# A pre-norm transformer block on one core: spline parts in the score banks, and the second norm's transpose on VectorE

## The chip, the cores and the metric

The kernel runs on one core of one Trainium2 chip. The metric is the device time of one execution in microseconds (us); a change is judged by the median of several runs of each kernel.

## The reference: what is computed

The input is 16 sequences of 256 tokens with 256 features, in 32-bit floats. One block of a transformer is computed: a layer norm, attention with 16 heads of 16 features each and a window mask, a residual sum, a second layer norm, and a gated feed-forward layer whose three weights (256 x 1024) are rebuilt from about two thousand control points each by cubic interpolation ("spline").

```python
n = layernorm(x)
q, k, v = n @ wq.T, n @ wk.T, n @ wv.T           # 16 heads of 16
s = q @ k.T * 16 ** -0.5                          # per head, 256 x 256
s = where(j - i > 16, -inf, s)
x = x + (softmax(s) @ v) @ wo.T
n = layernorm(x)                                  # the second norm
gate_w, up_w, down_w = (spline_reconstruct(cp) for cp in (gate_cp, up_cp, down_cp))
x = x + (silu(n @ gate_w.T) * (n @ up_w.T)) @ down_w.T
```

## The kernel before, in words

**Steps.** One sequence is one batch entry b, 0 to 15. The kernel walks through 20 steps s, and each step works on several sequences at different stages: the projections of b = s + 3, the row maxima of the scores of nb = s - 1, the exponentials and values of tb = s - 2, the output projection, residual and second norm of ob = s - 3, and most of the feed-forward layer of s - 4. All instructions of an engine are kept in program order (class `InOrder`; its helper line is line 88, so nearly all rows of the profile carry L88 and are told apart by their tiles). Nothing reorders them: the loop at the end of `block_kernel` writes the order out by hand, with gaps 1 to 7 of each step, at which `project(s, gap)` and `fill(s, gap)` put other work between the score stages. The dictionary `early` deals the work of the first steps (0 to 4) to those gaps: the first norm's transposes (`turn_a`), the projections and the weights' spline.

**Scores.** Two tiles, `scores0` and `scores1`, hold two PSUM banks each, so four of the eight banks. `inner` and `outer` fill them for four heads at a time: once without a mask for the maxima (TensorE, then VectorE's `find_max`, whose rows are `z` and `mx`), and once, for the sequence one step older, for the exponentials (ScalarE, rows `e`, then a mask by GpSimd). A step holds four `inner` and two `outer` stages. `turn_max` transposes the maxima (`pm`) and sends them into the q/k tile of the next step by SyncE's DMA queue.

**Other PSUM.** Pool `ps_f` (tag "f", two banks) holds the feed-forward products `pg`, `pu` and `pd`, and pool `ps_m` (tag "m", two banks) the projections `pq`, `pk`, `pv`, `py`, the values `po` and all transposes (`pta`, `ptf`, `pm`).

**The second norm.** `project_o` adds the attention's output to x (rows `x<-x,py`). `norm_stats` takes mean and variance on VectorE (`statsf`, `mvf`) and the inverse root on GpSimd (`rstdf`, power -0.5). `normed` writes `xnf` (two VectorE instructions). `turn_f` transposes it: `transposed` runs four TensorE transposes of 128 x 128 into a PSUM tile `ptf` and one ScalarE copy to `x2T`. `gate_up(b, 0)`, the next step's first feed-forward product, reads `x2T` whole as its moving operand; it stands at gap 7, the end of the step, and its first matmul is `pg`. In steps 4 to 12, TensorE has between the `outer` stage and that `pg`: `down(1)` (`pd`, 16 records), `ptf`, `project_v` (`pv`) and `pm`. From step 13 on there is no `project_v` any more, and `down` is dealt in halves (`fill`), so that `pd` for column block 0 has only one half ahead of `outer`. The sum `x<-x,pd` on VectorE releases each `pd` bank.

**The spline.** `spline(w, part)` makes half of one weight: four matmuls `pw` of 32 rows each into four PSUM banks (two of `ps_f`, two of `ps_m`), then per half a ScalarE copy of the first piece and a VectorE `copy_predicated` of the second over it. Six parts: (gate, 0), (up, 0), (gate, 1), (up, 1), (down, 0), (down, 1). Before, they stand at (step, gap) (0, 4), (1, 5), (1, 7), (2, 6), (2, 7) and (2, 7).

Of the kernel before, what the change touches and what calls it, by code (L numbers as in the profile page):

```python
# [11 lines left out]
F32 = mybir.dt.float32  # L12
BF16 = mybir.dt.bfloat16
AF = mybir.ActivationFunctionType
ALU = mybir.AluOpType
# [3 lines left out]
P = 128  # L19
B, S, DIM = 16, 256, 256  # L20
# [4 lines left out]
EPS = 1e-5  # L25
# [4 lines left out]
NPART = NROW // 2  # L30
# [63 lines left out]
def block_kernel(  # L94
# [14 lines left out]
    pe, dve, act, pool, sp = (  # L109
        InOrder(tc, e) for e in (nc.tensor, nc.vector, nc.scalar, nc.gpsimd, nc.sync)  # L110
    )

    const = ctx.enter_context(tc.tile_pool(name="const", bufs=1))
    sb = ctx.enter_context(tc.tile_pool(name="sb", bufs=2))
    sb1 = ctx.enter_context(tc.tile_pool(name="sb1", bufs=1))
    sb3 = ctx.enter_context(tc.tile_pool(name="sb3", bufs=3))
    sb4 = ctx.enter_context(tc.tile_pool(name="sb4", bufs=4))
# [4 lines left out]
    ps_f = ctx.enter_context(tc.tile_pool(name="ps_f", bufs=2, space=PSUM))  # L122
    ps_m = ctx.enter_context(tc.tile_pool(name="ps_m", bufs=2, space=PSUM))
# [48 lines left out]
    neghalf = const.tile([P, 2], F32, tag="neghalf", name="neghalf")  # L172
# [42 lines left out]
    xns, mxs, aus, aos, recs, x2s, x2Ts = ({} for _ in range(7))  # L215
    es, inters, qkcs = {}, {}, {}

    moments = {}

    def norm_stats(b, nm):  # L220
        stats = sb.tile([P, 2, 6], F32, tag=f"stats{nm}", name=f"stats{nm}{b}")
        mv = sb.tile([P, 2, 2], F32, tag=f"mv{nm}", name=f"mv{nm}{b}")
        for c in range(2):
            dve.bn_stats(stats[:, c, :], xs[b][:, c, :])
            dve.bn_aggr(mv[:, c, :], stats[:, c, :])
        rstd = sb4.tile([P, 2], F32, tag=f"rstd{nm}", name=f"rstd{nm}{b}")
        dve.tensor_scalar_add(rstd, mv[:, :, 1], EPS)
        pool.tensor_tensor(rstd, rstd, neghalf, ALU.pow)
        moments[b, nm] = mv, rstd

    def normed(b, nm):
# [9 lines left out]
    def copied(engine, dst, src):  # L241
        (act.copy if engine is act else dve.tensor_copy)(dst, src)

    def transposed(src, dst, nm, engine=act):

        pt = ps_m.tile([P, 2, S], F32, tag="m", name=f"p{nm}")
        for kc in range(2):
            for c in range(2):
                pe.transpose(
                    pt[:, kc, c * P : (c + 1) * P],  # L250
                    src[:, c, kc * P : (kc + 1) * P],
                    ident,
                )
        copied(engine, dst, pt)


    def stats_a(b):
        norm_stats(b, "a")
# [6 lines left out]
    def norm_a(b):  # L265
        xns[b] = normed(b, "a")

    def turn_a(b, engine=act):
        xTs[b] = sb3.tile([P, 2, S], F32, tag="xT", name=f"xT{b}")
        transposed(xns.pop(b), xTs[b], f"ta{b}", engine)  # L270
# [61 lines left out]
                    qks[b % NQK][32 * r : 32 * r + HD, :, gg::2, :], qkc[at : at + HD]  # L332
                )

    def project_v(b, engine=act, chunks=(0, 1)):
        pv = ps_m.tile([P, 2, DIM], F32, tag="m", name=f"pv{b}")
        for c in chunks:
            for kc in range(2):
                pe.matmul(
                    pv[:, c, :],  # L340
                    lhsT=xTs[b][:, kc, c * P : (c + 1) * P],
                    rhs=w_in["v"][:, kc, :],
                    start=(kc == 0),
                    stop=(kc == 1),
                )
        for c in chunks:
            to = vs[b % NQK][:, c, :, 0:HD]
            heads = pv[:, c, :].rearrange("p (h d) -> p h d", d=HD)
            if b < RAW:
                copied(engine, to, heads)  # L350
            else:
                act.activation(to, heads, AF.Copy, scale=factors[b][:, c : c + 1])
        if 1 in chunks:
            del xTs[b]
# [6 lines left out]
    tiles = [  # L361
        ps_s.tile([P, 2, 512], F32, tag=f"s{pr}", name=f"scores{pr}") for pr in range(2)
    ]
# [185 lines left out]
    def norm_f(b):  # L549
        x2s[b] = normed(b, "f")  # L550

    def turn_f(b):
        x2Ts[b] = sb.tile([P, 2, S], F32, tag="x2T", name=f"x2T{b}")
        transposed(x2s.pop(b), x2Ts[b], f"tf{b}")

    def product(out, lhsT, rhs, start, stop, columns=P):

# [66 lines left out]
            ALU.mult, ALU.mult,  # L624
        )

    def spline(w, part):
        at = slice(NPART * part, NPART * part + NPART)
        places = tab_in[:, NPART + P * part : NPART + P * part + P]

        pw = [
            pool_.tile([P, NPART], F32, tag=tag, name=f"pw{w}_{part}_{kc}_{piece}")
            for kc, (pool_, tag) in enumerate(((ps_f, "f"), (ps_m, "m")))
            for piece in range(2)
        ]
        for q in range(4):
            rows = slice(32 * q, 32 * q + 32)
            pe.matmul(
                pw[q], lhsT=places[rows], rhs=cp_in[rows, w, :], start=True, stop=True
            )  # L640
        for kc in range(2):
            first, other, where = pw[2 * kc], pw[2 * kc + 1], second_in[:, kc, at]
            if w < 2:
                to = (gateT, upT)[w][:, kc, at]
            else:

                to = downT[:, kc::2, NPART // 4 * part : NPART // 4 * (part + 1)]
                first, other, where = (
                    t.rearrange("p (o q) -> p q o", q=4) for t in (first, other, where)
                )  # L650
            act.copy(to, first)
            dve.copy_predicated(to, where, other)

    def do(stage, b, *args):
        if 0 <= b < B:
            stage(b, *args)

    parts = ((0, 0), (1, 0), (0, 1), (1, 1), (2, 0), (2, 1))
# [6 lines left out]
    def fill(s, gap):  # L665


        if s < B - AHEAD:
            order = (
                (1, gate_up, 1, 32), (3, gate_up, 2), (4, gate_up, 3, 32), (5, down, 0),  # L670
                (6, down, 1),
            )
        else:
            order = (
                (1, gate_up, 1, 32), (2, gate_up, 2), (3, gate_up, 3), (4, down, 0, 0, 32),
                (5, down, 0, 1), (6, down, 1, 0), (6.5, down, 1, 1),
            )
        for at, stage, *what in order:
            if at == gap:
                if s == B + 3 and stage is down:  # L680

                    if what[1] == 0:
                        down(B - 1, what[0])
                else:
                    do(stage, s - 4, *what)
        if gap == 7:
            do(gate_up, s - 3, 0)

    def part(i):
        spline(*parts[i])

    early = {
        (0, 1): ((stats_a, 1), (value_ones, 1)),
# [1 line left out]
            (norm_a, 1), (project_qk, 0), (spread, 0), (load_rest, 0), (coefficients, 0),  # L697
            (stats_a, 2), (scores_and_values, 2),
        ),
        (0, 4): ((turn_a, 1, dve), (project_v, 0, dve), (norm_a, 2), (part, 0)),  # L700
        (1, 1): ((turn_a, 2), (project_part, 1, 0), (stats_a, 3)),
        (1, 2): ((project_part, 1, 1), (spread, 1), (coefficients, 1)),
        (1, 3): ((project_qk, 2), (spread, 2), (norm_a, 3), (scores_and_values, 3)),
        (1, 4): ((project_v, 1), (stats_a, 4)),
        (1, 5): ((turn_a, 3), (part, 1), (norm_a, 4), (coefficients, 2)),
        (1, 6): ((project_qk, 3),),
        (1, 7): (
            (spread, 3), (stats_a, 5), (norm_a, 5), (project_v, 2), (part, 2),
            (scores_and_values, 4),
        ),  # L710
        (2, 1): ((turn_a, 4), (turn_a, 5), (scores_and_values, 5)),
        (2, 2): ((project_part, 4, 0), (stats_a, 6)),
        (2, 3): ((project_part, 4, 1), (spread, 4), (project_part, 5, 0)),
        (2, 4): ((norm_a, 6), (project_v, 3, act, (0,))),
        (2, 5): ((project_part, 5, 1), (spread, 5)),
        (2, 6): ((project_v, 3, act, (1,)), (part, 3)),
        (2, 7): ((part, 4), (part, 5)),
        (3, 1): ((turn_a, 6),),
        (3, 2): ((project_qk, 6), (spread, 6)),
        (3, 3): ((project_v, 4), (project_v, 5)),  # L720
        (3, 6): ((project_v, 6), (sum_weights, "q"), (sum_weights, "k")),
        (3, 7): ((center, "q"), (center, "k")),
        (4, 1): ((sum_weights, "v"), (center, "v")),
    }

    def project(s, gap):
# [22 lines left out]
    minus_ones(1)  # L749
    stats_a(0)  # L750
    norm_a(0)
    turn_a(0)
    for s in range(B + 4):
        nb, tb, ob = s - 1, s - 2, s - 3
        inner(nb, tb, 0)
        if ob < B - 1:
            do(values, ob, 1)
            do(gather, ob)
        project(s, 1)
        fill(s, 1)  # L760
        inner(nb, tb, 1)
        do(invert, ob)
        if s:
            do(load_x, s + 2 + AHEAD)
        project(s, 2)
        fill(s, 2)
        outer(nb, tb, 0)
        project(s, 3)
        fill(s, 3)
        inner(nb, tb, 2)  # L770
        do(values, tb, 0)
        project(s, 4)
        do(divide, ob)
        fill(s, 4)
        inner(nb, tb, 3)
        do(project_o, ob)
        do(stats_f, ob)
        project(s, 5)
        fill(s, 5)
        if s != 3:  # L780
            do(norm_f, ob)
        outer(nb, tb, 1)
        fill(s, 6)
        if s == 3:

            project(s, 6)
            norm_f(ob)
            turn_max(nb)
        do(turn_f, ob)
        if s != 3:  # L790
            project(s, 6)
        fill(s, 6.5)
        if tb == B - 1:
            values(tb, 1)
            gather(tb)
        if s != 3:
            do(turn_max, nb)
        project(s, 7)
        fill(s, 7)
# [30 lines left out]
```

## Time and profile before

| what | value |
|---|---|
| median of 3 runs | 651.25 us (650.94 to 652.86) |
| the profiled execution: its own time | 652.13 us |
| its span in the profile | 650.4 us |
| TensorE (PE), matmul busy | 642.7 us, 99% |
| VectorE (DVE) busy | 369.2 us, 57% |
| ScalarE (ACT) busy | 216.4 us, 33% |
| GpSimd (POOL) busy | 129.5 us, 20% |
| mean granted TensorE clock | 0.997 |

The span runs from the first to the last instruction of the program; 1.7 us of the profiled execution lie around it. Busy TensorE time is partly modelled: matmuls overlap, so what a stage costs is read from the starts of its first instruction and of the next stage's first one, not from the instructions' durations. A row of the timeline gives start, length, engine, operation, tiles written and read, count, and in brackets the idle time before it with what ended it.

### The profile page before, as it was taken

What the parts mean: (1) busy time and instruction counts of PE and PEld (TensorE: products, weight loads), DVE (VectorE), ACT (ScalarE), POOL (GpSimd) and SP (SyncE); (2) the same over time, 40 slices, a digit from 0 to 9 for tenths busy, and PEclk for the clock granted to TensorE, in tenths of its full rate; (3) what the DMA queues carried; (4) which work ended last, traced back from release to release, by engine and by line L of the source; (5) the groups of instructions that cost most, each with busy time, mean ns of one, the idle gap of its engine ahead of it and who ended that gap; (6) DMA issues with size and microseconds to landing.
All of it is one profiled execution on the core that took longest, in us unless ns stands there. A gap on an engine that the chain in (4) does not pass through costs nothing.

```text
span 650.4 us, 21144 instructions
## 1 busy us (share of the span) xinstructions
PE 642.7 (99%) x8740; PEld 477.3 (73%) x8740; DVE 369.2 (57%) x1483; ACT 216.4 (33%) x383; POOL 129.5 (20%) x254
## 2 busy tenths in 40 slices
PE   8999999999999999999999999999999999999998
PEld 7666667777778777787877778777777777777777
DVE  6785566646465664646566464655656565633342
ACT  1345543233332323333232332323333333333110
POOL 6232222111121211212112121211212030312000
PEclk9999899999999999999999999999999999999999
DMA  5843141414132131312213131210010101010100
GB/s 173 174 69 54 35 83 29 82 38 86 34 76 42 35 75 39 86 35 69 49 31 80 36 72 34 54 32 21 19 36 20 36 21 30 26 41 14 51 17 17
DMA packets 40768, 33.36 MB, mean 51 GB/s; under 512 B 10593, under 2 KB 40033, under 8 KB 40673
## 3 DMA queue, kind: packets, MB, share of 16 engines
q1 hardware_dynamic: 39392, 30.90, 21.7%
q8 instruction: 69, 1.13, 0.8%
q10 hardware_dynamic: 1280, 1.11, 0.6%
q14 instruction: 27, 0.21, 0.3%
HBM read 14.42 MB, written 4.47 MB: 29 GB/s over the span
## 4 chain that ended last, share of the span: by engine, by line
PE 96%; DMA 1%; DVE 1%; ACT 1%; issue 1%; POOL 0%; SPq 0%; ACTq 0%
PE pg L88 18%; PE pd L88 17%; PE pu L88 17%; PE scores L88 15%; PE po L88 7%; PE py L88 5%; PE pq L88 4%; PE pk L88 4%; PE pv L88 4%; PE pw L88 1%; PE ptf L88 1%; DMA qk<-qkc 1%; DMA x<-x 1%; PE pm L88 1%; PE pta L88 0%
## 5 line engine op out<-in xcount | busy, mean ns | idle before, releaser
L88 ACT ACTIVATE e<-scores 128x512 f32<-128x512 f32 (+1 forms) x192 | 117.5, 615 | 268.9 <-PE scores L88 222.6
L88 DVE CUSTOM_DVE_ANT_0 z<-scores,mask 128x144 bf16<-128x144 f32 (+1 forms) x512 | 154.7, 362 | 56.0 <-PE scores L88 33.3
L88 POOL TENSOR_SCALAR_AFFINE_SELECT e<-e 128x224 f32<-128x224 f32 (+1 forms) x192 | 93.8, 489 | 403.0 <-ACT e L88 402.6
L88 PE MATMUL pg<-x2T,gateT 128*32 128x256 f32 (+1 forms) x1112 | 124.0, 381 | 0.7 <-ACT x2T L88 0.7
L88 PE MATMUL pu<-x2T,upT 128*32 128x256 f32 (+1 forms) x1112 | 121.4, 379 | 0.0
L88 PE MATMUL pd<-downT,inter 128*128 128x256 f32 (+2 forms) x672 | 119.1, 376 | 0.0
L88 DVE SCALAR_TENSOR_TENSOR th<-th,pg 128x512 f32<-128x512 f32 x64 | 44.0, 688 | 113.4 <-ACT th L88 113.4
L88 PE MATMUL scores<-qk 17*64 17x144 f32 (+7 forms) x4096 | 106.5, 317 | 1.2 <-ACT e L88 1.1
L88 PEld LDWEIGHTS pd<-downT,inter 128*128 128x128 f32 (+1 forms) x672 | 93.3, 167 | 15.4 <-DVE th L88 0.3
L88 PEld LDWEIGHTS pu<-x2T,upT 128*32 128x32 f32 (+1 forms) x1112 | 85.3, 132 | 25.2
L88 PEld LDWEIGHTS pg<-x2T,gateT 128*32 128x32 f32 (+1 forms) x1112 | 81.8, 132 | 25.7 <-DVE inter L88 1.5
L88 PEld LDWEIGHTS scores<-qk 17*64 17x64 f32 (+1 forms) x4096 | 68.8, 131 | 39.1 <-issue 33.1
L88 ACT ACTIVATE th<-pg 128x512 f32<-128x512 f32 x64 | 38.2, 597 | 67.6 <-PE pg L88 67.0
L88 DVE TENSOR_TENSOR inter<-th,pu 128x512 f32<-128x512 f32 x64 | 44.0, 688 | 26.2 <-PE pu L88 26.2
L88 PE MATMUL po<-e,v 128*32 128x256 f32 (+1 forms) x1024 | 51.2, 342 | 0.0
L88 PEld LDWEIGHTS po<-e,v 128*32 128x32 f32 x1024 | 30.0, 111 | 24.3 <-issue 13.5
L88 DVE DVE_READ_ACCUMULATOR2_ANT mx<- 128x1 f32 x512 | 42.5, 83 | 0.1
L88 DVE TENSOR_TENSOR x<-x,pd 128x256 f32<-128x256 f32 (+1 forms) x33 | 13.6, 412 | 41.4 <-PE pd L88 41.4
L88 PE MATMUL pq<-xT,wq 128*128 128x256 f32 x128 | 31.7, 390 | 0.7 <-ACT xT L88 0.7
L88 PE MATMUL py<-wo,ac 128*128 128x256 f32 x128 | 31.9, 392 | 0.0
L88 PE MATMUL pv<-wv,xT 128*128 128x256 f32 x128 | 31.0, 385 | 0.4 <-ACT qkc L88 0.4
L88 PE MATMUL pk<-xT,wk 128*128 128x256 f32 x128 | 30.6, 381 | 0.0
(69 smaller groups left out, 384.0 us busy)
## 6 DMA issues: line engine op xcount, KB each, us to landing
qk<-qkc SPq DMA_DIRECT2D x124, 64.0 KB
x<-x SPq DMA_DIRECT2D x16, 256.0 KB
ac<-au SPq DMA_DIRECT2D x128, 32.0 KB
rb<-rd SPq DMA_DIRECT2D x32, 128.0 KB
out<-x SPq DMA_DIRECT2D x15, 256.0 KB
xT<-xT SPq DMA_DIRECT2D x9, 256.0 KB
fa<-ra SPq DMA_DIRECT2D x9, 128.0 KB
qk<-mxT SPq DMA_DIRECT2D x64, 4.0 KB
```

The source lines that it names most:

```text
L88: return self.tc.keep_in_program_order(fn(*args, **kwargs))
```

## The change

Three edits, in one diff.

1. **The second norm's transpose.** For b = 1 to 14, `turn_f` no longer uses TensorE, PSUM and ScalarE. VectorE transposes `xnf` in 32 by 32 blocks, straight into `x2T`: 16 instructions per sequence, each reading 32 partitions (q) and writing 32 partitions (m), 128 elements per partition. Four of them (m = 0) stand right behind `xnf` and ahead of `outer`'s maxima; the other twelve stand behind those maxima. To make room, `norm_f` goes ahead of `fill(s, 5)`, and `turn_f` ahead of `fill(s, 6)`: the sums `x<-x,pd` come behind `xnf` and the transposes on VectorE. The order of TensorE's remaining instructions there is as before. Sequences 0 and 15 keep TensorE's transposes.
2. **Spline parts and the first steps.** A part can now be made in the four score banks ("ssss") or in a chosen mix ("fmmf"). The parts stand at (0, 4), (1, 5), (1, 7) "ssss", (2, 7) "ssss", (2, 7) "fmmf" and (3, 7) "ssss"; in (2, 7) half of a `project_v` goes between the two. `project_v` of 4 and 5 moves from (3, 3) to (2, 6), (2, 7) and (3, 6), the centering of the weights from (3, 6) to (4, 1) to (3, 2) and (3, 3).
3. **The very first norm** takes the inverse root column by column, and sequence 0's transposes are copied out in two halves, by ScalarE and then VectorE. All transposes on TensorE go chunk by chunk.

```diff
     def transposed(src, dst, nm, engine=act):
         pt = ps_m.tile([P, 2, S], F32, tag="m", name=f"p{nm}")
-        for kc in range(2):
-            for c in range(2):
+        for c in range(2):
+            for kc in range(2):
                 pe.transpose(
...
-        copied(engine, dst, pt)
+        if engine:
+            copied(engine, dst, pt)
+        else:
+            for kc, engine in enumerate((act, dve)):
+                copied(engine, dst[:, kc, :], pt[:, kc, :])
...
-    def turn_f(b):
-        x2Ts[b] = sb.tile([P, 2, S], F32, tag="x2T", name=f"x2T{b}")
-        transposed(x2s.pop(b), x2Ts[b], f"tf{b}")
+    def turn_f(b, early=False):
+        if early or not 0 < b < B - 1:
+            x2Ts[b] = sb.tile([P, 2, S], F32, tag="x2T", name=f"x2T{b}")
+        if 0 < b < B - 1:
+            src = x2s[b].rearrange("p c (kc d) -> p c kc d", kc=2)
+            dst = x2Ts[b].rearrange("p kc (c t) -> p c kc t", c=2)
+            for m in (0,) if early else (32, 64, 96):
+                for q in range(0, P, 32):
+                    dve.transpose(
+                        dst[m : m + 32, :, :, q : q + 32], src[q : q + 32, :, :, m : m + 32]
+                    )
+            return
+        transposed(x2s.pop(b), x2Ts[b], f"tf{b}", act if b else None)
...
-    def spline(w, part):
+    def spline(w, part, home="ffmm"):
...
+            tiles[q // 2][:, q % 2, :]
+            if tag == "s"
+            else (ps_f if tag == "f" else ps_m).tile(
+                [P, NPART], F32, tag=tag, name=f"pw{w}_{part}_{q}"
+            )
+            for q, tag in enumerate(home)
...
         (1, 7): (
-            (spread, 3), (stats_a, 5), (norm_a, 5), (project_v, 2), (part, 2),
-            (scores_and_values, 4),
+            (spread, 3), (stats_a, 5), (part, 2, "ssss"), (norm_a, 5), (project_v, 2),
         ),
...
-        (2, 6): ((project_v, 3, act, (1,)), (part, 3)),
-        (2, 7): ((part, 4), (part, 5)),
+        (2, 6): ((project_v, 3, act, (1,)), (project_v, 4)),
+        (2, 7): ((part, 3, "ssss"), (project_v, 5, act, (0,), "f"), (part, 4, "fmmf")),
         (3, 1): ((turn_a, 6),),
-        (3, 2): ((project_qk, 6), (spread, 6)),
-        (3, 3): ((project_v, 4), (project_v, 5)),
-        (3, 6): ((project_v, 6), (sum_weights, "q"), (sum_weights, "k")),
-        (3, 7): ((center, "q"), (center, "k")),
-        (4, 1): ((sum_weights, "v"), (center, "v")),
+        (3, 2): ((project_part, 6, 0), (sum_weights, "q"), (center, "q")),
+        (3, 3): (
+            (project_part, 6, 1), (spread, 6), (sum_weights, "k"), (sum_weights, "v"),
+            (center, "k"), (center, "v"),
+        ),
+        (3, 6): ((project_v, 6), (project_v, 5, act, (1,))),
+        (3, 7): ((part, 5, "ssss"),),
...
         project(s, 5)
-        fill(s, 5)
         if s != 3:
             do(norm_f, ob)
+        if 0 < ob < B - 1:
+            turn_f(ob, True)
+        fill(s, 5)
         outer(nb, tb, 1)
-        fill(s, 6)
...
-        do(turn_f, ob)
+        if ob < B - 1:
+            do(turn_f, ob)
+        fill(s, 6)
+        if ob == B - 1:
+            turn_f(ob)
```

More of the change, by code (lines that the diff above doesn't have):

```diff
@@ L218, in block_kernel, with inverse_root @@
     moments = {}
+    def inverse_root(to, variances, power):
+        dve.tensor_scalar_add(to, variances, EPS)
+        pool.tensor_tensor(to, to, power, ALU.pow)
     def norm_stats(b, nm):
@@ L222, in norm_stats @@
         mv = sb.tile([P, 2, 2], F32, tag=f"mv{nm}", name=f"mv{nm}{b}")
+        rstd = sb4.tile([P, 2], F32, tag=f"rstd{nm}", name=f"rstd{nm}{b}")
         for c in range(2):
@@ L225, in norm_stats @@
             dve.bn_aggr(mv[:, c, :], stats[:, c, :])
-        rstd = sb4.tile([P, 2], F32, tag=f"rstd{nm}", name=f"rstd{nm}{b}")
-        dve.tensor_scalar_add(rstd, mv[:, :, 1], EPS)
-        pool.tensor_tensor(rstd, rstd, neghalf, ALU.pow)
+            if b == 0 and nm == "a":
+                inverse_root(rstd[:, c : c + 1], mv[:, c, 1:2], neghalf[:, 0:1])
+        if not (b == 0 and nm == "a"):
+            inverse_root(rstd, mv[:, :, 1], neghalf)
         moments[b, nm] = mv, rstd
@@ L333, in spread, with project_v @@
                 )
-    def project_v(b, engine=act, chunks=(0, 1)):
-        pv = ps_m.tile([P, 2, DIM], F32, tag="m", name=f"pv{b}")
+    def project_v(b, engine=act, chunks=(0, 1), home="m"):
+        if home == "s":
+            pv = tiles[1][:, 1, :].rearrange("p (c d) -> p c d", d=DIM)
+        else:
+            pv = (ps_m if home == "m" else ps_f).tile([P, 2, DIM], F32, tag=home, name=f"pv{b}")
         for c in chunks:
@@ L631, in spline @@
         pw = [
-            pool_.tile([P, NPART], F32, tag=tag, name=f"pw{w}_{part}_{kc}_{piece}")
-            for kc, (pool_, tag) in enumerate(((ps_f, "f"), (ps_m, "m")))
-            for piece in range(2)
+            tiles[q // 2][:, q % 2, :]
[4 more added lines that the diff above has]
+            for q, tag in enumerate(home)
         ]
@@ L687, in fill, with part @@
             do(gate_up, s - 3, 0)
-    def part(i):
-        spline(*parts[i])
+    def part(i, home="ffmm"):
+        spline(*parts[i], home)
     early = {
@@ L699, in block_kernel @@
         ),
-        (0, 4): ((turn_a, 1, dve), (project_v, 0, dve), (norm_a, 2), (part, 0)),
+        (0, 4): ((turn_a, 1, dve), (project_v, 0, dve, (0, 1), "s"), (norm_a, 2), (part, 0)),
         (1, 1): ((turn_a, 2), (project_part, 1, 0), (stats_a, 3)),
@@ L705, in block_kernel @@
         (1, 5): ((turn_a, 3), (part, 1), (norm_a, 4), (coefficients, 2)),
-        (1, 6): ((project_qk, 3),),
+        (1, 6): ((scores_and_values, 4), (project_qk, 3)),
         (1, 7): (
-            (spread, 3), (stats_a, 5), (norm_a, 5), (project_v, 2), (part, 2),
-            (scores_and_values, 4),
+            (spread, 3), (stats_a, 5), (part, 2, "ssss"), (norm_a, 5), (project_v, 2),
         ),
@@ L751, in block_kernel @@
     norm_a(0)
-    turn_a(0)
+    turn_a(0, None)
     for s in range(B + 4):
```

## The prediction

> **What bounds the kernel now.** I read the page's busy times first, then the chain that ended last, then the timeline of one step in the middle and one near the end.
>
> ```profile
> PE 642.7 (99%) x8740; PEld 477.3 (73%) x8740; DVE 369.2 (57%) x1483; ACT 216.4 (33%) x383; POOL 129.5 (20%) x254
> ...
> PE 96%; DMA 1%; DVE 1%; ACT 1%; issue 1%; POOL 0%; SPq 0%; ACTq 0%
> ```
>
> TensorE is the chain: whatever leaves its queue shortens the time, and whatever makes it wait lengthens the time one for one. VectorE's 57% is an average; what counts is how much room it has just ahead of the one matmul that will wait for it. First, the end of a middle step (step 5, sequence 2), TensorE and then VectorE:
>
> ```profile
> 164.78 1.14 PE L88 MATMUL scores<-qk 16*64 16x80 f32 x64
> 165.85 3.72 PE L88 MATMUL pd<-downT,inter 128*128 128x256 f32 x16
> 169.41 0.60 PE L88 MATMUL ptf<-ident,xnf 128*128 128x128 f32 x4
> 169.84 1.89 PE L88 MATMUL pv<-wv,xT 128*128 128x256 f32 x8
> 171.57 0.38 PE L88 MATMUL pm<-ident,mx 128*16 128x128 f32 x2
> ```
> ```profile
> 163.36 0.17 DVE L88 TENSOR_SCALAR rstdf<-mvf 128x2 f32<-128x2 f32 x1
> 164.88 0.42 DVE L88 TENSOR_TENSOR x<-x,pd 128x256 f32<-128x256 f32 x1 [1.36 <-PE pd L88]
> 165.22 0.73 DVE L88 TENSOR_SCALAR xnf<-x,mvf,rstdf 128x256 f32<-128x256 f32 x2
> 166.18 0.31 DVE L88 CUSTOM_DVE_ANT_0 z<-scores,mask 128x144 bf16<-128x144 f32 x1 [0.23 <-PE scores L88]
> ```
>
> The transposes hold TensorE from 169.41 to 169.84: 0.44 us. The reader `pg` starts at 171.79. The eight maxima of `outer` run from 166.18 to 168.10 (1.92 us), 3.69 us before that `pg`. Now step 13 (sequence 10), the first with the other deal:
>
> ```profile
> 466.02 1.14 PE L88 MATMUL scores<-qk 16*64 16x80 f32 x64
> 467.09 1.99 PE L88 MATMUL pd<-downT,inter 128*128 128x256 f32 x8
> 468.92 0.60 PE L88 MATMUL ptf<-ident,xnf 128*128 128x128 f32 x4
> 469.35 1.89 PE L88 MATMUL pd<-downT,inter 128*128 128x256 f32 x8
> 471.08 0.38 PE L88 MATMUL pm<-ident,mx 128*16 128x128 f32 x2
> ```
> ```profile
> 467.30 0.73 DVE L88 TENSOR_SCALAR xnf<-x,mvf,rstdf 128x256 f32<-128x256 f32 x2 [0.49 <-POOL rstdf L88]
> 467.95 0.30 DVE L88 CUSTOM_DVE_ANT_0 z<-scores,mask 128x144 bf16<-128x144 f32 x1
> ```
>
> Here the maxima start right behind `xnf` and end at 469.86, only 1.44 us before `pg` (471.30): VectorE has no idle time ahead of them, and TensorE has no `pv` to cover what follows them.
>
> **Transposes off TensorE.** Removed per sequence: 0.44 us of TensorE and a 0.59 us ScalarE copy. The copy is worth nothing: ScalarE is 33% busy and `pg` waits for `x2T` only once (0.7 us). Fourteen sequences give 14 x 0.44 = 6.1 us at most. *A rule beside it:* the Trainium skill, "TensorE: Matmul & The Clock Gate", section "Part 4: PE-mode transpose", gives about 275 ns per transpose inside a kernel. The row's own mean is 273 ns, but four of them move the next matmul by 0.44 us, since they overlap; by durations the gain would read 14 x 4 x 0.275 = 15.4 us. The starts decide.
>
> **Transposes onto VectorE.** Added per sequence: 16 instructions of 128 elements per partition, price T each from start to start. No row shows one, nor any instruction that follows another without a wait while it reads other partitions. From below: the two `xnf` start 0.324 us apart for 256 elements, `find_max` costs 1.04 ns per element (0.345 less 0.229 us over 112), so 128 fewer leave T = 0.19; by `find_max` itself (0.229 at 144) it is 0.21. From above: alone, a 128-wide row lasts 0.288 us (`x<-x,pd` 128x128), and an instruction that waits for its predecessor's end starts 0.034 later (`statsf` to `mvf`): 0.32. I take 0.31: 409 ns of one `xnf` less 128 x 1.04 is 0.276, plus 0.034. I go to the upper side because every overlapped pair in the trace stays on the same 128 partitions, and these sixteen change partitions each time. *The rule against this change:* the same skill, "VectorE: DVE Perf Modes", section "Two Vector instructions with no wait between them", says that an instruction whose input or output starts in another group of 32 partitions than before is held until all earlier ones have finished. All but one of the sixteen would be held; the page calls it a model, and no run here shows it yet. By it T is on the upper side, without it on the lower.
>
> *Middle steps (sequences 1 to 9, nine of them).* GpSimd's root ends at 164.30, so `xnf` can start at 164.33 once the `pd` sum is behind it, and ends at 165.06; transposes start at 165.10. Then 4T, the `pd` sum (0.34 to the next start), the maxima (1.92), 12T, and 0.05 to TensorE: x2T is ready at 167.41 + 16T. `pg` could start at 171.79 - 0.44 = 171.35. So there is no wait up to T = 0.246, and the step breaks even at 0.274. With T = 0.31: 172.37, which is 0.58 us later than before, nine times: +5.2. With T = 0.21: -0.44 each, -4.0.
>
> *Late steps (10 to 13, four of them).* `xnf` cannot start before 467.30 (it waits for GpSimd). Then 468.07 + 4T + 0.34 + 1.91 + 12T + 0.05 = 470.37 + 16T, against 471.30 before. With 0.31: 475.33, +4.03 each, +16.1. With 0.21: 473.73, +2.43 each, +9.7. It loses for every T over 0.058: in these steps the change cannot pay.
>
> *Sequence 14* has no maxima: `xnf` ends at 598.14, ready at 598.56 + 16T against `pg` at 602.03: +1.5 with 0.31, -0.1 with 0.21.
>
> Sum of the transposes: 5.2 + 16.1 + 1.5 = **+22.8 us** at 0.31; +5.6 at 0.21; +4.0 at 0.19.
>
> What waits behind them: the `pd` sum, so its bank (next used by `pu`, 1.7 us behind `pg`: in time) and the output DMA. Behind that on SyncE's queue stand the four `mxT` DMAs, issued from 172.87, the first landing at 174.46, for scores at 175.3. The DMA would issue about 172.8 and `mxT` 0.5 later, but the scores move with `pg`: nothing added. ScalarE's second `e` and GpSimd's mask come up to 1.6 us later and are read a step later.
>
> **Spline parts and first steps.** Where the profile shows their cost:
>
> ```profile
> 60.98 1.13 PE L88 MATMUL pw<-cp_in,tab_in 32*128 32x512 f32 x6
> 62.30 1.12 PE L88 MATMUL pw<-cp_in,tab_in 32*128 32x512 f32 x2 [0.18 <-ACT v L88]
> ...
> 63.66 4.28 PE L88 MATMUL pw<-cp_in,tab_in 32*128 32x512 f32 x16
> 67.87 1.40 PE L88 MATMUL scores<-qk 16*64 16x208 f32 x32
> 69.20 2.84 PE L88 MATMUL po<-e,v 128*32 128x256 f32 x32
> ```
> ```profile
> 61.00:68.00 7.00, 6.78 (x35) 2.40 (x42) 4.49 (x16) 4.53 (x9) 1.05 (x2) 1.00 0.49 74
> 68.00:72.00 4.00, 4.00 (x65) 1.89 (x64) 3.27 (x15) 1.20 (x3) 0.76 (x2) 0.57 0.02 6
> ```
>
> The second fence is busy time by window; the seventh value is the granted clock. With four free banks a part runs in two rounds, each 0.535 us (60.98 to 61.52): 1.07. The three parts took 2.36 + 4.21 = 6.57, so 3.4 us are waits for banks that ScalarE and VectorE had not emptied. Right behind, the clock falls to 0.57 and scores, `po` and `pta` take 4.68 us instead of 2.9: 1.8 more. Part 2 (40.00 to 41.91) and a gap ahead of its `pv` lose 1.16. Sequence 0's `pg` at 94.05 waits 1.0 us for `x2T`, which a part at (3, 7) would fill. Together 7.3 us. Given back: the fourth matmul of "fmmf" waits for a ScalarE copy of `pv` in the same bank (some 0.65), and the scores of step 3, now earlier, meet the `mxT` DMAs, which still queue behind eight `qk<-qkc` DMAs (some 0.7). I take **-5.5 us**, between -7.3 and -3 (clock dip stays). The root by columns gives 0 to 0.1: GpSimd's root takes 0.70 us each time, now twice in a row, and the two half copies read one PSUM bank one after the other.
>
> **Sum.** +22.8 - 5.5 = +17.3. The profiled execution took 652.13 us (span 650.4), 0.9 over the median; so 669.4 there, and **668.6** against the median of 651.25.
>
> **Rivals.**
> - *The transposes overlap (T = 0.21):* the middle steps gain 4.0, the late steps still lose 9.7, and the first steps pay it back: +5.6 - 5.5, about 651.3. For it: all unblocked rows overlap by 0.07 to 0.09 us. Against it: the change of partitions.
> - *Faster.* The same mechanism at its cheapest, T = 0.19 at VectorE's queue between `xnf` and `pg`, with the first steps' 7.3 whole: +4.0 - 7.3 = -3.3, 648.0. It decides from T at or under 0.2 and at least 6 us at the start.
> - *A transpose costs as much as a 256-wide row* (0.44: two passes for 4 bytes): 16T = 7.04, so +2.66 x 9, +6.1 x 4 and +3.6, 51.9 in all; 698. Nothing in the trace speaks for it.
> - *The start saves nothing*, because the score banks are emptied too late for the next scores: at T = 0.31, 674. Against: behind each "ssss" part stands a `pv`, another part or `gate_up`, 1.0 to 3.5 us.
>
> **How the numbers follow.** The bound for no change is 0.3%, 2 us (649.3 to 653.2), about what a measurement of this kernel can tell. Forecast with T of 0.26 to 0.36, a weak start included (660 to 680): 0.55. Overlap (649.3 to 655): 0.22, of which 0.17 is within the bound. Faster: 0.15. Two passes: 0.08. So faster 0.15, same 0.17, slower 0.68. The range goes from 648.5 (overlap, and part of the faster case) to 680.
>
> **What would show it.** Right: transposes starting some 0.31 us apart; `pg` of sequences 1 to 13 waiting for VectorE's `x2T`, about 1 us in middle steps and 4.5 in late ones; TensorE's share under 99%; no clock dip near 68 us, and sequence 0's `pg` some 5 us earlier than 94.05. Wrong: transposes 0.2 apart and no wait in middle steps; a wait on another engine; or a start that moves little.

## The result, and the profile after

The changed kernel takes **685.91 us** (median of 6 runs, 682.48 to 686.59) against 652.03 us (6 runs) for the kernel before beside it: ratio 1.0504, 95% interval 1.0481 to 1.0528 (ratios come from the single runs of both kernels and can differ a little from the quotient of the medians). Two executions of the experiments below, one of `late_twelve` (912.5 us) and one of `spread_late` (1291.5 us), took far longer than the others of their kernel and are left out. The profiled execution took 682.48 us (span 680.8, mean granted clock 0.985), 30.4 us more than that of before.

The page, engines and chain, and the first two waits of TensorE (us in total, times, longest):

```profile
PE 643.4 (95%) x8684; PEld 475.6 (70%) x8684; DVE 437.7 (64%) x1710; ACT 207.8 (31%) x369; POOL 128.8 (19%) x255
...
PEclk9999999999999999999999999999798989989999
...
PE 74%; DVE 19%; issue 2%; POOL 1%; SPq 1%; DMA 1%; ACT 1%; ACTq 0%; POOLq 0%; DVEq 0%
...
L88 DVE STREAM_TRANSPOSE x2T<-xnf 32x128 f32<-32x128 f32 x224 | 67.8, 303 | 3.6
```
```profile
PE pg L88 <- DVE x2T L88: 24.9, 14, 3.4
PE pm L88 <- DVE mx L88: 3.7, 4, 0.9
```

TensorE's share of the chain fell from 96% to 74%, VectorE's rose from 1% to 19%. TensorE has 56 instructions fewer (14 x 4, as meant) and is still busy for 0.7 us longer. Busier with less work: the clock row says why. Its digits drop to 7 and 8 in the last third.

A middle step, VectorE and then TensorE (step 5, sequence 2, as shown of before):

```profile
161.65 1.24 DVE L88 STREAM_TRANSPOSE x2T<-xnf 32x128 f32<-32x128 f32 x4
...
165.21 3.79 DVE L88 STREAM_TRANSPOSE x2T<-xnf 32x128 f32<-32x128 f32 x12
```
```profile
165.95 1.89 PE L88 MATMUL pv<-wv,xT 128*128 128x256 f32 x8
167.68 0.38 PE L88 MATMUL pm<-ident,mx 128*16 128x128 f32 x2
169.06 1.13 PE L88 MATMUL pg<-x2T,gateT 128*128 128x256 f32 x4 [0.99 <-DVE x2T L88]
```

The `ptf` row is gone, and a wait of 0.99 us stands in its place. The transposes start 0.312 to 0.321 us apart. From `pg` to `pg` a middle step takes 38.90 us, 0.81 more than before.

A late step (step 13, sequence 10), VectorE and then TensorE:

```profile
470.49 0.73 DVE L88 TENSOR_SCALAR xnf<-x,mvf,rstdf 128x256 f32<-128x256 f32 x2 [0.81 <-POOL rstdf L88]
471.26 1.24 DVE L88 STREAM_TRANSPOSE x2T<-xnf 32x128 f32<-32x128 f32 x4
...
474.81 3.79 DVE L88 STREAM_TRANSPOSE x2T<-xnf 32x128 f32<-32x128 f32 x12
```
```profile
470.28 3.72 PE L88 MATMUL pd<-downT,inter 128*128 128x256 f32 x16
474.93 0.38 PE L88 MATMUL pm<-ident,mx 128*16 128x128 f32 x2 [0.93 <-DVE mx L88]
478.75 3.75 PE L88 MATMUL pg<-x2T,gateT 128*128 128x256 f32 x8 [3.45 <-DVE x2T L88]
482.30 2.41 PE L88 MATMUL pu<-x2T,upT 128*128 128x256 f32 x6
```

From `xnf` on VectorE works without a pause, and TensorE waits twice: 0.93 us ahead of `pm` (four transposes now stand ahead of the maxima) and 3.45 ahead of `pg`. Then comes what the prediction did not have: the eight matmuls of `pg` take 3.54 us to the start of `pu`, where the middle step's take 1.83. TensorE by windows: start and end, length, then TensorE's busy time (with its records), the granted clock, and the share and the GB/s of the DMA engines:

```profile
473.98:477.39 3.41, 0.40 (x3) 1.00 0.00 0
477.39:480.80 3.41, 2.05 (x5) 0.50 0.22 77
480.80:484.22 3.42, 3.42 (x9) 0.50 0.03 7
484.22:487.63 3.41, 3.41 (x72) 1.00 0.00 0
```

Busy for only 0.40 of 3.41 us, then two stretches of 3.41 us at half clock. The same follows the other three late waits: 3.41 us at half clock from 518.35, 6.83 from 555.89, 3.41 from 596.86, 20.5 us in all. These starts lie whole multiples of 3.413 us apart (12, 11 and 12 of them), as if a clock of its own decided every 3.41 us. Before the change, these steps ran at full clock.

What the late steps grew by, `pg` to `pg`: 4.36, 7.03, 5.85 and 6.93 us; sequence 14 added 3.32. (The stretches behind a wait count in the step that follows, so the first has none yet.) The nine middle steps added 7.3, and the new start had gained 4.4 in this execution (sequence 1's `pg` stands 3.56 us earlier, its own wait's 0.8 included).

### The profile page after: what moved, and what is told of

It reads as the page before. It is cut to its first block, busy times and chain, and to the rows that moved or that the text cites. A ratio compares the mean times of both kernels' runs of the same rounds, so it can differ in the third digit from the quotient of the medians.

```text
span 680.8 us, 21254 instructions
## 1 busy us (share of the span) xinstructions
PE 643.4 (95%) x8684; PEld 475.6 (70%) x8684; DVE 437.7 (64%) x1710; ACT 207.8 (31%) x369; POOL 128.8 (19%) x255
## 4 chain that ended last, share of the span: by engine, by line
PE 74%; DVE 19%; issue 2%; POOL 1%; SPq 1%; DMA 1%; ACT 1%; ACTq 0%; POOLq 0%; DVEq 0%
PE pg L88 18%; PE pu L88 16%; PE scores L88 13%; DVE x2T L88 9%; PE po L88 7%; PE py L88 5%; PE pq L88 4%; PE pk L88 4%; PE pd L88 4%; DVE z L88 3%; DVE x L88 2%; DVE xnf L88 1%; DVE statsf L88 1%; POOL rstdf L88 1%; SPq L88 1%
## 5 line engine op out<-in xcount | busy, mean ns | idle before, releaser
L88 PE MATMUL pg<-x2T,gateT 128*32 128x256 f32 (+1 forms) x1112 | 131.7, 389 | 24.9 <-DVE x2T L88 24.9
L88 PEld LDWEIGHTS pg<-x2T,gateT 128*32 128x32 f32 (+1 forms) x1112 | 86.2, 136 | 55.1 <-issue 17.8
L88 PE MATMUL pu<-x2T,upT 128*32 128x256 f32 (+1 forms) x1112 | 123.3, 381 | 0.0
L88 PEld LDWEIGHTS pu<-x2T,upT 128*32 128x32 f32 (+1 forms) x1112 | 86.9, 134 | 26.1
L88 DVE STREAM_TRANSPOSE x2T<-xnf 32x128 f32<-32x128 f32 x224 | 67.8, 303 | 3.6
L88 PE MATMUL pv<-wv,xT 128*128 128x256 f32 x120 | 29.1, 384 | 0.2 <-issue 0.2
```

The costliest lines, as they stand in the source:

```text
L88: return self.tc.keep_in_program_order(fn(*args, **kwargs))
```

## The experiments

**Theory A:** the loss is VectorE's sixteen transposes, each held until the one before has ended because it starts in other partitions, and on top of the waiting TensorE's clock halves behind the long late waits. **Rivals:** 0.31 us is the transpose's own price; the late loss is waiting alone; the new start lost its gain. Ratios are to the kernel before in the same group of runs (medians 651.81, 651.37 and 651.19 us).

### Apart: the start alone, the transposes alone, the middle steps alone

`start_only` is the changed kernel with this edit:

```diff
-        if 0 < b < B - 1:
...
-            return
         transposed(x2s.pop(b), x2Ts[b], f"tf{b}", act if b else None)
```

and the loop order of before. `turn_only` is the kernel before with the change's `turn_f` and loop. `middle_only` is the changed kernel with `0 < b < B - 1` narrowed to `0 < b < 10`; the later steps have the loop order of before.

> The changed kernel with the second norm transposed by TensorE again, in the loop order of before; only the start (score banks for spline parts, steps dealt anew, root by columns) stays changed. Theory A (the loss is all in VectorE's transposes and what they do to TensorE, and the start keeps most of its gain): 4.4 us under the kernel before, read from where sequence 1's gate and up stood in the changed kernel (3.56 earlier, after a wait of 0.82 that goes away), so about 647.6; no stretch at half clock near 68 us. The prediction's own term was 5.5 under, 646.5. Rival (the start only moves its waits, and later steps give them back): within 1.5 us of the kernel before, 650.5 or more.

Measured: 650.07 us (647.74 to 651.88), ratio 0.9969 (0.9949 to 0.9989): 1.7 us gained. No stretch near 68 us, but the gain is less than half of either number expected, and it lies between theory and rival.

> The kernel before with VectorE's transposes alone; the start is that of before. Theory A: the changed kernel's time plus the 4.4 us that the start gave: 687 to 691, that is 34.8 to 38.3 over the kernel before, with four or more stretches at half clock behind sequences 10 to 13. Rival (TensorE's clock has no part in it, and the late steps were slow for the new start's sake): the prediction's 22.8 over, about 675. If the two parts act on each other, the sum of this kernel's and the start's differences misses the changed kernel's by more than 2 us.

Measured: 687.96 us (687.38 to 688.40), ratio 1.0558 (1.0537 to 1.0579): 36.2 over. Its trace shows the same waits as the changed kernel's, 24.9 us in 14 and 3.7 in 4, and six stretches at half clock behind sequences 10 to 13, which also speaks against the start as their cause. The two parts add up: 36.2 - 1.7 = 34.5, and the whole change cost 33.9.

> VectorE transposes for sequences 1 to 9 only; 10 to 14 go back to TensorE with their old order; the start stays changed. Theory A: the middle steps lose 0.81 each, 7.3 in all, on top of the start's 4.4 under: about 655, 3 over the kernel before, and no stretch at half clock, since their waits are 1 us. The prediction's term for them was 5.2: 652.8. Rival (the whole loss belongs to the transposes wherever they stand, 30 us over 14 sequences, 2.2 each): some 667.

Measured: 656.13 us (653.95 to 662.96), ratio 1.0074 (1.0044 to 1.0105), 6.1 over the start alone; in the traces each of these steps takes 0.82 more, 7.4 in nine, which the interval (some 2 us to each side) allows. As theory A has it. There is one stretch at half clock, at 91 us in the start, none at the waits of 1 us.

### The price: the same partitions, and the input kept

`same_parts` reads and writes the same group of 32 partitions, which then changes only with every fourth instruction; `input_kept` exchanges the loops:

```diff
-    dst[m : m + 32, :, :, q : q + 32], src[q : q + 32, :, :, m : m + 32]
+    dst[m : m + 32, :, :, q : q + 32], src[m : m + 32, :, :, q : q + 32]
```
```diff
-            for m in (0,) if early else (32, 64, 96):
-                for q in range(0, P, 32):
+            for q in (0,) if early else (32, 64, 96):
+                for m in range(0, P, 32):
```

> The changed kernel with the same sixteen instructions of the same shape, but each writes the group of 32 partitions that it reads (blocks stay in their own group, so the second norm is turned wrongly and the output is not the reference's). Twelve of the sixteen then follow an instruction in the same partitions; four change. Theory A (0.317 us because each instruction starts in other partitions than the one before and waits for its end): twelve at about 0.20 to 0.23 and four at 0.317, some 1.1 to 1.4 us less in each sequence; middle waits go, late waits fall to about 2.2, no half clock: 659 to 664. Rival (0.31 us is the transpose's own price): the changed kernel's time, 685 to 687.

Measured: 662.33 us, ratio 1.0172 (1.0149 to 1.0195). In its trace, VectorE in the middle step:

```profile
160.65 0.88 DVE L88 STREAM_TRANSPOSE x2T<-xnf 32x128 f32<-32x128 f32 x4
...
163.70 2.68 DVE L88 STREAM_TRANSPOSE x2T<-xnf 32x128 f32<-32x128 f32 x12
```

Twelve take 2.68 us where they took 3.79. Start to start: 0.235 behind the first of a group, then 0.193, 0.193, and 0.272 where the group changes. So 0.31 isn't the transpose's price. The middle steps now pay: most take 37.65 us, 0.44 less than before the change, just what the transposes took of TensorE. The time came out as expected, but in part by luck: waits of about 2.3 us stayed in the late steps, and each was still followed by one stretch at half clock:

```profile
462.91:466.32 3.41, 0.97 (x5) 1.00 0.00 0
466.32:469.74 3.42, 3.09 (x7) 0.50 0.23 79
469.74:473.15 3.41, 3.41 (x50) 1.00 0.02 5
```

> The changed kernel with its two loops exchanged: four transposes in a row read the same 32 partitions, while each writes other ones (before, each read others and four wrote the same). Theory A as the page of the skill has it (a change of the input's or of the output's group is enough): 0.317 again, the changed kernel's time within 2 us. Rival (only a change of the input's group holds an instruction): twelve of sixteen overlap, as in the kernel that keeps both: 659 to 664.

Measured: 684.14 us, ratio 1.0503 (1.0469 to 1.0536); the changed kernel's was 1.0504. Starts 0.312 to 0.320 us apart. Here a change of the output's group alone holds an instruction, as in the changed kernel a change of the input's alone does. The Trainium skill, "VectorE: DVE Perf Modes", section "Two Vector instructions with no wait between them", calls this a model: held whenever the input or the output starts in another group of 32 partitions. All three orders agree with it here.

### The clock: the wait filled, and the wait shortened

`filled` puts matmuls that nobody reads into the late waits:

```diff
         project(s, 7)
+        if 10 <= ob < B - 1:
+            keep = ps_m.tile([P, 2 * S], F32, tag="m", name=f"keep{ob}")
+            for _ in range(14 if nb < B else 8):
+                pe.matmul(keep[:, 0:P], lhsT=ident, rhs=ident, start=True, stop=True)
         fill(s, 7)
```

> The changed kernel with 14 matmuls of the identity (8 in the last of these steps) put on TensorE between the transposed maxima and the late sequences' (10 to 14) gate and up; nothing reads them. TensorE has more to do and the chain through VectorE is as long as before. Theory A (a wait of about 3.4 us brings TensorE's clock to half for one or two stretches of 3.41 us): no stretch at half clock behind them, and 8 to 13 us under the changed kernel, about 673 to 678. Rival (the late loss is waiting alone): the changed kernel's time or more, 686 to 688.

Measured: 674.16 us (673.44 to 676.39), ratio 1.0347 (1.0321 to 1.0373): 0.0157 of 651 us, some 10 us, under the changed kernel (give or take 2 by the intervals), with more work on TensorE. Its late step, in which the 14 matmuls stand as 28 records:

```profile
476.68 0.38 PE L88 MATMUL pm<-ident,mx 128*16 128x128 f32 x2 [0.94 <-DVE mx L88]
476.90 3.29 PE L88 MATMUL keep<-ident 128*128 128x128 f32 x28
480.41 1.99 PE L88 MATMUL pg<-x2T,gateT 128*128 128x256 f32 x8 [0.23 <-DVE x2T L88]
482.24 1.03 PE L88 MATMUL pu<-x2T,upT 128*128 128x256 f32 x4
```

`pg` takes 1.83 us to `pu`, not 3.54, and no stretch at half clock is left in these steps. Three of its four runs have a mean clock of 1.000, where the changed kernel's have 0.980 to 0.985. VectorE's chain is as long as before, so this kernel also shows what the waiting alone costs: a late step takes 37.18 us, 4.27 over the kernel before, and sequence 14's 1.80.

`late_twelve` and `late_eight` leave out four or eight transposes in the late steps; ScalarE writes those rows early. The diff is that of `late_twelve`; `late_eight` has 64 in place of 96 and `(32,)` in place of `(32, 64)`:

```diff
+            if early and b >= 10:
+                act.copy(x2Ts[b][96:P], gateT[96:P, :, 0:S])
-            for m in (0,) if early else (32, 64, 96):
+            for m in (0,) if early else (32, 64) if b >= 10 else (32, 64, 96):
```

> The changed kernel, but in sequences 10 to 14 VectorE leaves out four of its sixteen transposes (the last 32 features of each half; those rows are filled early by a ScalarE copy of weights, so these sequences' feed-forward outputs are not the reference's). Theory A (price per instruction, and a clock that falls only behind a long wait): the late waits fall from 3.45 to about 2.2 us, 4 x 1.27 + 1.27 = 6.3 less, and with them go the stretches at half clock, 10 to 13 us: 666 to 670. Rival (no part of the clock): 6.3 less only, 679.6. Rival (the wait is not the transposes' count but something behind them): 684 to 686.

Measured: ratio 1.0384 (1.0346 to 1.0421), three runs of 674.77, 675.53 and 678.58 us: between theory and rival, and so against theory A in its first form. A further run shows the clock in its profile.

> The kernel that leaves out four late transposes once more, for a profile that can be read (sequences 10 to 14, the last 32 features of each half hold weights in place of the norm). Its time of 675 us lies between theory A's 666 to 670 and the 679.6 without the clock. If the clock is set by stretches of 3.41 us, each late wait of about 2.2 us is followed by one stretch at half clock, not two and not none; if theory A's first form holds there is none, and the missing gain must be a wait elsewhere.

Measured: 675.74 us. The waits are 2.2 us now, and one stretch at half clock follows each of the four, as the windows around the first show (ahead of the clock now the busy times of all five: TensorE's matmuls and weight loads, VectorE, ScalarE, GpSimd):

```profile
475.12:478.54 3.42, 0.64 (x4) 0.12 (x2) 3.29 (x18) 1.01 (x2) 0.64 (x1) 1.00 0.00 0
478.54:481.95 3.41, 3.09 (x7) 2.52 (x8) 0.60 (x2) 0.00 (x0) 0.00 (x0) 0.50 0.23 80
481.95:485.36 3.41, 3.41 (x50) 2.39 (x52) 1.53 (x3) 0.76 (x2) 0.00 (x0) 1.00 0.02 5
```

So a single gap of 3.4 us isn't needed.

> As the kernel that leaves out four, but eight of the sixteen transposes are left out in sequences 10 to 14 (the last 64 features of each half; those rows hold a ScalarE copy of weights, so these sequences' feed-forward outputs are not the reference's). The runs so far change theory A: waits of 2.3 us halved the clock too, and the profiles so far show the clock set anew every 3.41 us, half after a stretch of 3.41 us with over some 1.5 us without a matmul. So the late waits of 3.45 - 8 x 0.317 = 0.9 us should halve nothing: five times 2.5 less of waiting, and 10 to 13 us of half clock less: 660 to 663. Rival (the clock has no part, or any wait in these steps halves it): 12.7 us less only, 673; if one stretch of 3.41 us stays in each step, some 667 to 670.

Measured: 662.89 us (662.41 to 663.60), ratio 1.0173 (1.0148 to 1.0198), by the ratios 0.033 or some 21 us under the changed kernel. Eight transposes less in five steps are at most 12.7 us of waiting; the other 9, found by subtraction, are the clock's, and the trace has 17 us less at half clock than the changed kernel's. Three of the four late steps run at full clock. The fourth shows the rule best:

```profile
577.12:580.53 3.41, 1.58 (x8) 1.00 0.00 0
580.53:583.95 3.42, 3.42 (x10) 0.50 0.26 87
```

Here no wait is longer than 0.93 us, but two of them fall into one stretch: 1.83 us without a matmul in 3.41. In the other late steps the stretches' borders part them, at most 1.40 us fall into one, and the clock stays.

### Towards a faster kernel

`twelve_middle` is `middle_only` with the last 32 of each 128 tokens turned by TensorE (VectorE's instructions stand in the order of `input_kept`):

```diff
+                pe.transpose(
+                    pt[:, kc, c, :], src[96:P, c, kc * P : (kc + 1) * P], ident[96:P, 96:P]
+                )
```

> As the kernel with transposes on VectorE for sequences 1 to 9, but there VectorE turns only the first 96 of each 128 tokens (12 instructions), and TensorE turns the other 32 in four small transposes that one short ScalarE copy empties. Theory A (the wait is the queue of instructions behind one another, so four fewer at 0.317 take 1.27 us off and end a wait of 0.99): no wait left, and TensorE's four small transposes cost between 0.11 (a quarter of 0.44) and 0.44 us: 0 to 3 us under the kernel with the start alone, so 644.6 to 647.6. Rival (four transposes of 32 columns cost as much as four of 128, and the ScalarE copy is late): at or over the start alone, 648 to 650.

Measured: 650.03 us, ratio 0.9992 (0.9971 to 1.0014), no better than the start alone. The wait is gone, as theory A had it; the gain isn't there. TensorE in this kernel's middle step, and in the start alone's:

```profile
165.28 0.43 PE L88 MATMUL ptf<-ident,xnf 32*128 32x32 f32 x4
165.64 1.99 PE L88 MATMUL pv<-wv,xT 128*128 128x256 f32 x8
167.47 0.38 PE L88 MATMUL pm<-ident,mx 128*16 128x128 f32 x2
```
```profile
166.46 0.60 PE L88 MATMUL ptf<-ident,xnf 128*128 128x128 f32 x4
166.90 1.89 PE L88 MATMUL pv<-wv,xT 128*128 128x256 f32 x8
168.63 0.38 PE L88 MATMUL pm<-ident,mx 128*16 128x128 f32 x2
```

A quarter of the tokens takes 0.36 us to the start of `pv` where all of them take 0.44, and `pv` behind it takes 1.83 in place of 1.73. The step is 0.12 us longer than with four whole transposes.

`spread_late` moves sequence 6's eight DMAs of queries and keys in `start_only`:

```diff
-            (project_part, 6, 1), (spread, 6), (sum_weights, "k"), (sum_weights, "v"),
+            (project_part, 6, 1), (sum_weights, "k"), (sum_weights, "v"),
...
-        (3, 7): ((part, 5, "ssss"),),
+        (3, 7): ((part, 5, "ssss"), (spread, 6)),
```

> The kernel with the start alone, with sequence 6's eight DMAs of queries and keys issued at the end of step 3 in place of its middle. In every kernel with the new start, ScalarE's first e of step 3's last scores begins 0.9 to 2.3 us after those scores end (0.06 in the kernel before), one of these DMAs lands 3.7 us after its issue, and the maxima's transposes wait up to 1.8 us. Theory S (these DMAs, now beside step 3's scores, hold them up): the hold-up goes, gate and up of sequence 0 start near 90.5, and the time is 1 to 2 us under the kernel with the start alone (650.1), 648 to 649. Rival (the hold-up has another cause, and the DMAs only suffer from it): 649.5 to 650.7, with the same hold-up in the trace.

Measured: 648.32 us (646.60 to 651.77), ratio 0.9956 (0.9939 to 0.9973): by its median the fastest kernel of the study, under both kernels of the change. ScalarE ahead of step 3's last scores, in `start_only` and in `spread_late`:

```profile
87.97 0.65 ACT L88 ACTIVATE e<-scores 128x576 f32<-128x576 f32 x1 [4.01 <-PE pv L88]
```
```profile
84.72 0.65 ACT L88 ACTIVATE e<-scores 128x576 f32<-128x576 f32 x1 [1.49 <-PE scores L88]
```

2.3 us behind those scores' end in the first, 0.2 in the second, and sequence 0's `pg` starts at 89.92 in place of 92.57. The median lies where theory S had it, but by the ratios this kernel is only 0.8 us under `start_only`, and the intervals overlap. So theory S isn't shown; against it, the profiles of `late_eight` and `late_twelve_2`, with the DMAs in the old place, have no hold-up either (0.2 and none), so it comes and goes with the execution, and TensorE's records name no cause for it.

## Why the prediction was wrong, step by step

It said 668.6 us, range 648.5 to 680. The direction, the bound and the waits were right; what a wait costs was not, and the time is 6 us over the range's end.

- *Bounds and transposes off TensorE:* right. `pg` waits for VectorE's `x2T` wherever the change put it, and TensorE lost exactly the 56 instructions. One reading was off without consequence: the mean of the `ptf` row is 275 ns; 273 is its median.
- *T = 0.31:* right, 0.312 to 0.321, and so was the ground for the upper side: with the partitions kept, 0.193, next to the lower bound of 0.19.
- *Middle steps, +0.58 each:* +0.81 in the trace, 2.1 us more over nine. 16 x 0.007 = 0.11 is T; another 0.10 is that `pg` takes 1.83 us to `pu` behind a wait, 1.73 without.
- *Late steps, +4.03 each, and sequence 14, +1.5:* the waits were right (4.27 and 1.80 with the clock kept up in `filled`); the step that failed is the one that turned them into time. The text took a wait to cost its own length, "one for one". Here each late wait also brought 3.41 to 6.83 us at half clock. **This is the missing term**: about 10 us, by `filled` against the changed kernel; 9 by `late_eight`. Without it the time would be some 676 us, inside the range. No bound of the range had it, though the working had priced such a dip at 68 us at 1.8.
- *Start, -5.5:* -1.7 (-3.3 to -0.7). Two of its steps failed. The dip near 68 us was counted as the kernel's, but 16 of the 25 runs of the kernel before that ran beside `start_only` have a mean clock of 0.999 or more: it belongs to some executions only, and the median already lacks it. And the hold-up at step 3's scores came to 0.9 to 2.3 us in seven of the nine readable traces with the new start and the DMAs in their place, where 0.7 was allowed. TensorE waits up to 1.8 us ahead of `pm` there, and in two of these traces (`middle_only`, 1.68 us, and `input_kept`, 1.53) a stretch at half clock near 91 us followed. Nor is the new start at full clock more often: only 3 of the 12 runs of `start_only` have 0.999 or more, with a median of 647.84 us, 2.8 under the 650.63 of the 16 such runs of the kernel before. The other nine have 0.995 to 0.997; where their stretches at half clock lie, no trace of them shows. How the missing 3.8 us divide among these causes stays open.

The sum in medians: 17.3 predicted, plus 10 of clock, 3.8 of the start, 2.1 of middle steps and 1.3 of late waits and sequence 14, is 34.5; measured 33.9.

Of what would show it: transposes 0.31 apart, waits of 1 us in the middle and 4.4 (0.93 + 3.45) in late steps, a share of 95% and no dip near 68 all came; sequence 0's `pg` came 2.8 us earlier (91.24), not 5. What the list lacked is the granted clock in the late steps.

## What to carry to other kernels

Price a wait of the engine that is the bound by more than its length: here waits that left TensorE without matmuls for 1.83 us or more of a 3.41 us stretch cost up to 1.7 us (half of 3.41) again for each stretch at half clock behind them. Shorten such a wait, split it, or fill it with matmuls nobody reads. Before moving work like this to VectorE in pieces of 32 partitions, price it held (0.31 us for these transposes), not overlapped (0.19), unless its pieces can keep their partitions. A clock dip in one profile is counted as recoverable only if the clocks of the other runs show it too.

## What the runs showed of the hardware

- **When the clock halves.** In the late steps, a stretch of 3.41 us on a fixed grid with 1.83 us or more without a matmul was always followed by one at half clock, and one with 1.40 or less never, while the clock was full. Between lie cases of both kinds: 1.55 and 1.70 near 88 us were followed by half clock; 1.54 there, 1.52 at sequence 10 and 1.59 to 1.75 at sequence 14 were not. It isn't idle time alone: before the change, a stretch with next to none (65.02 to 68.43, mostly `pw` of 32 rows) was followed by half too, and so were two in the first steps with 1.13 (`filled`, from 14.75) and 1.10 (`late_twelve_2`, from 14.32), where `same_parts` with 1.06 kept the full clock. From half, a stretch with 0.81 or more idle stayed at half, with 0.43 or less it went back. The Trainium skill, "TensorE: Matmul & The Clock Gate", section "Why this matters for your kernels", asks for no gaps over about 3 us between matmuls. These runs show a stricter limit: two gaps of 0.93 and 0.90 us in one stretch sufficed. The same page's window of 3413 ns, which runs freely (section "What's actually happening"), agrees with the distances between the stretches.
- **Where the grid falls decides the price.** The same late wait of 3.45 us brought one stretch or two, as the borders cut it: the stretches behind one late wait lengthen the step up to the next `pg`, and these are 2.8, 1.6, 2.7 and 1.5 us longer than in `filled` (two stretches, one, two, one).
- **A small transpose is hardly cheaper.** Four of 32 tokens took 0.36 us on TensorE, four of 128 tokens 0.44, and the matmul group behind the small ones lost 0.10.
